# Layer norms' inverse deviation: ScalarE square root and VectorE reciprocal, or a ScalarE copy and a GpSimd power

## The chip, the core and the metric

The kernel runs on one core of a Trainium2 chip. It is written in Bass with the Tile framework. The engines are named as the profile names them: PE (TensorE matmul) and PEld (its weight loads), DVE (VectorE), ACT (ScalarE), POOL (GpSimd) and SP (SyncE, which issues DMAs). The metric is the device time of one execution in microseconds, the median of several runs.

## The reference

A batch of 4 images of 192 channels and 64 x 64 pixels, all in 32-bit floats, goes through four layers:

```python
# layer 0: per pixel over the 192 channels
xn = layer_norm(x)                          # (x - mu) * rsqrt(var + 1e-5) * g + b
q = deform_conv(xn, w_p, b_p, w_d)          # offsets by a 3x3 convolution, bilinear gather of 9 taps
k, v = l2norm(split(qkv(xn)))
x = x + proj(softmax(q @ k.T * temperature) @ v)    # attention over channels, 6 heads
x = x + gelu(layer_norm(x) @ w_fc1 + b) @ w_fc2 + b
# layer 1: attention over all 4096 pixels, 96 channels
x = x + W(softmax(theta(x).T @ phi(x)) @ g(x).T)
# layer 2: 8x8 windows at stride 6, 6 heads
y = qkv(layer_norm(x))
x = x + hft(proj(fold(window_attention(y))))        # hft: sigmoid of a depthwise 3x3, times its input
z1, z2 = split(gelu(fc1(layer_norm(x))))
x = x + fc2(z1 * dwconv3(layer_norm(z2)))
# layer 3: a depthwise 3x3 with weights computed from the image's mean
out = depthwise(x, weights(mean(x)))
```

Every `layer_norm` takes mean and variance over the channels of one pixel. These five norms (layer 0's first and second, layer 2's first, second and the one of its gate `z2`) are what the change touches.

## The kernel before

Channels lie on the partitions, pixels along the free dimension. The channels of a pixel are thus summed by a matmul with a matrix of 1/192 (or 1/384), and each norm is the same chain of steps over a block of pixels:

- PE: mean into PSUM (`pm`); DVE: difference `d`; ACT: square `sq`.
- PE: `variances`, four groups of matmuls that put the variance of a quarter of the block into 32 partitions each (`pv`), so that 512 pixels make a tile of 128 x 128.
- ACT: `r = sqrt(pv + eps)`, read from PSUM, written to SBUF.
- DVE: `r = 1 / r`.
- PE: `spread_quarters`, which spreads `r` back over all partitions (`pb`); DVE: `d * pb`.

`layer_norm_steps` (L354) yields after each step: MEAN, DIFFERENCE, SQUARE, VARIANCE (after ACT's square root) and INVERSE (after the reciprocal), so that callers can place the steps among other work. It serves layer 0's first norm (`offsets`, tiles `r_l`, 8 blocks per image, 128 columns) and layer 2's first norm (`windows`, tiles `r_l2n`, 11 rows of windows per image, mostly 96 columns). `norm_steps` in `mlp0` (tiles `r_l0m`, 8 per image, 128 columns), `pair_norm_steps` (tiles `r_l2n` at L1365, 4 per image, 256 columns) and `gate_variance` in `mlp` (tiles `rz`, 8 per image, 128 columns, with the reciprocals at L1661 and L1667) are the same chain for other layouts.

The images run through these stages, in program order:

- `offsets(0)` and `gather(0)`: layer 0's first norm, the offset convolution and 297 indirect DMAs issued by POOL (L572), with the offsets of image 1 woven into it (`woven=True`); then `mlp0(0)` alone.
- For each image b: `keys` (for b = 1 and 2 with the offsets of image b + 1 woven in), `layer1` with the gather of image b + 1 woven in, `windows`, and `rest`: `project`, `mlp` and `layer3` of image b, into which `mlp0(b + 1)` is woven in parts. For the last image nothing is woven in.

The Tile framework's planner orders instructions by their costs and priorities, except under `tc.manual_schedule()`, where each engine keeps the order of the program. `windows` and `mlp` (with the parts of `mlp0` that run within it) are written under it. In `windows`, three groups of windows make a row. In group 0 the norm of the row after next runs up to its square; after group 1's second pair come its variance, square root and reciprocal (`norm(wr + 2, INVERSE)`, L1284); group 2 begins with the scores of the next group (L1112), and then spreads the result (`norm(wr + 2)`, L1267). In POOL's queue lie the copies into `xs`, `qs`, `ks`, `qw`, `xw` (L1064 to L1091) and the additions at L1199. In `mlp`, the order around the gate norm is

```python
gate_difference(hi)
widen(j, (1,))          # matmuls, then Gelu on ACT
gate_variance(lo)       # variances, then the square root on ACT
gate_square(hi)
widen(j, (2,))
...                     # depthwise taps on DVE
nc.vector.reciprocal(r[lo], r[lo])
gate_variance(hi)
... # means of the next pair's norm
nc.vector.reciprocal(r[hi], r[hi])
```

The compiler puts a table load (ACT_TABLE_LOAD) ahead of an ACT instruction whose function is not in the table set that is loaded. The functions used here are Square, Sqrt, Identity, Copy, Gelu, Exp and Sigmoid.

Of the kernel before, what the change touches and what calls it, by code (L numbers as in the profile page):

```python
# [12 lines left out]
AF = mybir.ActivationFunctionType  # L13
ALU = mybir.AluOpType
# [65 lines left out]
def conv_seq_kernel(ctx: ExitStack, tc: tile.TileContext, a, out: bass.AP):  # L80
    nc = tc.nc
# [11 lines left out]
    def const(shape, name):  # L93
        return wpool.tile(shape, F32, tag=name, name=name)
# [8 lines left out]
    V, VW = {}, {}  # L103
# [53 lines left out]
    for w in range(2):  # L157
        to = pixels[:, :, STRIDE * w : STRIDE * w + WS]
        nc.gpsimd.tensor_add(to, to, ident[:, bass.ts(w, WS * WS)].rearrange("p (r c) -> p r c", c=WS))
    eps = const([128, 1], "eps")  # L160
    nc.gpsimd.memset(eps, 1e-5)
    headmask = const([P, P], "headmask")
# [188 lines left out]

    MEAN, DIFFERENCE, SQUARE, VARIANCE, INVERSE = range(5)

    def layer_norm_steps(src, n, dst, sb, ps, name, affine=None, rows=None, tag="v", bufs=2, own=""):  # L354

        pm = ps.tile([128, 512], F32, tag="n", name=f"pm_{name}")[:P, :n]
        for k in range(2):
            nc.tensor.matmul(pm, lhsT=mean192, rhs=src[:, k, :], start=k == 0, stop=k == 1)  # L360
        yield MEAN
        d = sb.tile([P, 2, 512], F32, tag=f"ln_d{own}", name=f"d_{name}", bufs=bufs)[:, :, :n]
        dst = d if dst is None else dst
        nc.vector.tensor_tensor(d, src, pm.unsqueeze(1).to_broadcast([P, 2, n]), ALU.subtract)
        yield DIFFERENCE
        sq = sb.tile([P, 2, 512], F32, tag=f"ln_sq{own}", name=f"sq_{name}")[:, :, :n]
        nc.scalar.activation(sq, d, AF.Square)
        yield SQUARE
        pv = ps.tile([128, 512], F32, tag=tag, name=f"pv_{name}", bufs=1)[:, 0 : n // 4]
        variances(pv, sq, mean192)  # L370
        r = sb.tile([128, 128], F32, tag="ln_r", name=f"r_{name}", bufs=2)[:, 0 : n // 4]
        nc.scalar.activation(r, pv, AF.Sqrt, bias=eps)
        yield VARIANCE
        nc.vector.reciprocal(r, r)
        yield INVERSE
        pb = spread_quarters(r, n, P, ps, name)
        for k in range(2):
            of, to, r = d[:, k, :], dst[:, k] if rows else dst[:, k, :], pb
            if rows:
                of, r = (t.rearrange("p (r c) -> p r c", r=rows) for t in (of, r))  # L380
            if affine is None:
                nc.vector.tensor_tensor(to, of, r, ALU.mult)
            else:
                nc.vector.tensor_tensor(of, of, r, ALU.mult)
                nc.scalar.activation(to, of, AF.Identity, bias=affine[1][:, k], scale=affine[0][:, k])
        return dst
# [18 lines left out]
    def offsets(b, pool, kept=None, woven=False):  # L405
# [19 lines left out]
        with ExitStack() as s:  # L425
            sb = s.enter_context(pool_of(name="l0a", bufs=1 if woven else 2))
            s1 = s.enter_context(pool_of(name="l0a1", bufs=1))
            ps = s.enter_context(pool_of(name="l0aps", bufs=2, space=PSUM))
            for i in range(NCH):
                xi = sb.tile([P, 2, CN], F32, tag="xi", name=f"xi_{b}_{i}", bufs=2)  # L430
                nc.sync.dma_start(out=xi, in_=given(b)[:, :, bass.ts(i, CN)])
                layer_norm(
                    xi, CN, xnv[:, :, 1 + 8 * i : 9 + 8 * i, 1:65], sb, ps, f"l0_{b}_{i}",
                    affine=(V["l0_g1"], V["l0_b1"]), rows=8,
                )
                yield

# [257 lines left out]
    def mlp0(b, m2, pool, sb, ps):  # L695
# [58 lines left out]
        def norm_steps(x, i):  # L754

            pm = ps.tile([128, CN], F32, tag="n", name=f"pm_l0m_{b}_{i}")
            nc.tensor.matmul(pm, lhsT=mean_all[:, 0, :], rhs=x[:, 0:CN], start=True, stop=False, skip_group_check=True)
            for q in range(2):
                nc.tensor.matmul(
                    pm[:, bass.ts(q, HN)], lhsT=mean_all[:, 1 + q, :], rhs=x[:, CN:], start=False, stop=True,  # L760
                    skip_group_check=True,
                )
            yield MEAN
            d = sb.tile([M, 3 * HN], F32, tag="wide_d", name=f"d_l0m_{b}_{i}", bufs=2)
            over(d, x, pm, ALU.subtract)
            yield DIFFERENCE
            sq = sb.tile([M, 3 * HN], F32, tag="wide_sq", name=f"sq_l0m_{b}_{i}")
            nc.scalar.activation(sq, d, AF.Square)
            yield SQUARE
            pv = ps.tile([128, CN], F32, tag="v", name=f"pv_l0m_{b}_{i}", bufs=1)[:, 0:128]  # L770
            for j in range(4):
                to = pv[32 * j : 32 * j + 32, :]
                nc.tensor.matmul(to, lhsT=mean_all[:, 0, 0:32], rhs=sq[:, bass.ts(j, 128)], start=True, stop=False)
            for j in range(4):
                to, at = pv[32 * j : 32 * j + 32, :], CN + 128 * (j % 2)
                nc.tensor.matmul(to, lhsT=mean_all[:, 1 + j // 2, 0:32], rhs=sq[:, at : at + 128], start=False, stop=True)
            r = sb.tile([128, 128], F32, tag="ln_r", name=f"r_l0m_{b}_{i}", bufs=2)
            nc.scalar.activation(r, pv, AF.Sqrt, bias=eps)
            yield VARIANCE
            nc.vector.reciprocal(r, r)  # L780
            yield INVERSE
            over(d, d, spread_quarters(r, CN, M, ps, f"l0m_{b}_{i}"), ALU.mult)
            return d
# [555 lines left out]
    def pair_norm_steps(x, j, sb, ps, name):  # L1339

        lo, hi = of_pair(x, j)
        pms = [ps.tile([128, CN], F32, tag="n", name=f"pm_{name}_{h}") for h in range(2)]
        for h in range(2):
            nc.tensor.matmul(pms[h], lhsT=mean_all[:, 0, :], rhs=lo[:, h], start=True, stop=False)
        for h in range(2):
            nc.tensor.matmul(pms[h], lhsT=mean_all[half(h), 0, :], rhs=hi[half(h)], start=False, stop=True)
        yield MEAN
        d = sb.tile([M, 3, CN], F32, tag="ln_d", name=f"d_{name}")
        for h in range(2):
            nc.vector.tensor_tensor(d[:, h], lo[:, h], pms[h], ALU.subtract)  # L1350
            nc.vector.tensor_tensor(d[half(h), 2], hi[half(h)], pms[h][half(h)], ALU.subtract)
        yield DIFFERENCE
        sq = sb.tile([M, 3, CN], F32, tag="ln_sq", name=f"sq_{name}")
        nc.scalar.activation(sq, d, AF.Square)
        yield SQUARE

        pv = ps.tile([128, CN], F32, tag="v", name=f"pv_{name}", bufs=1)[:, 0:HN]
        for k in range(2):
            for g in range(4):
                nc.tensor.matmul(  # L1360
                    pv[32 * g : 32 * g + 32, :], lhsT=mean_all[:, (1 + g // 2) * k, 0:32],
                    rhs=sq[:, 2 if k else g // 2, bass.ts(g % 2, HN)], start=k == 0, stop=k == 1,
                )
        r = sb.tile([128, HN], F32, tag="ln_r2", name=f"r_{name}")
        nc.scalar.activation(r, pv, AF.Sqrt, bias=eps)  # L1365
        yield VARIANCE
        nc.vector.reciprocal(r, r)
        yield INVERSE
        for h in range(2):
            pb = ps.tile([128, CN], F32, tag="n", name=f"pb_{name}_{h}")  # L1370
            for g in range(2):
                nc.tensor.matmul(pb[:, bass.ts(g, HN)], lhsT=spread[:, 2 * h + g, :], rhs=r, start=True, stop=True)
            nc.vector.tensor_tensor(d[:, h], d[:, h], pb, ALU.mult)
            nc.vector.tensor_tensor(d[half(h), 2], d[half(h), 2], pb[half(h)], ALU.mult)
        return d
# [120 lines left out]
    def mlp(b, x, sums, sb, ps, taps, hn):  # L1496


        with ExitStack() as s:
# [6 lines left out]
            n = 2 * 3 * (UR + 2) * (W + 2)  # L1506
# [8 lines left out]
            r, sqs, accs = {}, {}, {}  # L1515
# [33 lines left out]
            def gate_variance(i):  # L1549
                pv = ps.tile([128, 512], F32, tag="n", name=f"pvz_{b}_{i}")[:, 0:128]  # L1550
                variances(pv, sqs.pop(i), mean384)
                r[i] = s1.tile([128, 128], F32, tag="zr", name=f"rz_{b}_{i}", bufs=2)
                nc.scalar.activation(r[i], pv, AF.Sqrt, bias=eps)

            def gate_scale(i):
                z2 = z2s.pop(i)
# [69 lines left out]
            with tc.manual_schedule():  # L1626
                for j in range(pairs):
                    lo, hi, upper, lower = 2 * j, 2 * j + 1, j - 1, j - 2
# [29 lines left out]
                    widen(j, (2,))  # L1658
                    if upper >= 0:
                        upper_taps(upper, 1)  # L1660
                    nc.vector.reciprocal(r[lo], r[lo])  # L1661
                    gate_variance(hi)
                    norm = None
                    if j + 1 < pairs:
                        norm = pair_norm_steps(x, j + 1, sb, ps, f"l2n2_{b}_{j + 1}")
                        links(norm, MEAN)
                    nc.vector.reciprocal(r[hi], r[hi])  # L1667
                    if norm is not None:
                        links(norm, SQUARE)
                    if upper >= 0:  # L1670
# [187 lines left out]
    with ExitStack() as s:  # L1858
        sb = s.enter_context(pool_of(name="l0first", bufs=1))
# [137 lines left out]
```

## Time and profile before

| what | value |
|---|---|
| time, median of 3 runs | 6844.52 us (6835.98 to 6856.77) |
| profiled execution: span | 6951.6 us |
| profiled execution: time | 6951.6 us (the span, no other time is on record for it) |
| mean granted TensorE clock | 0.938 |
| instructions | 115213 |
| HBM | 628 MB read, 106 MB written |

The profile is of one execution. PE, DVE, ACT and POOL are busy for a share of the span; register, branch, semaphore and DMA-issuing instructions are not counted. Groups of instructions are shown with their line, engine, operation, names of tiles (output<-inputs) and shapes, then their busy time, the mean duration of one in ns, and the idle time of the engine just before them with what ended it. The chain of waits is followed back from the last instruction, at each step to what released it. The stages of the first image lie at 0 to 632 us (offsets and gather), 632 to 858 (`mlp0`), 858 to 1615 (`keys`, `layer1`), 1615 to 1898 (`windows`) and 1898 to 2392 (`rest`).

### The profile page before, as it was taken

To read this page: it belongs to the slowest core of one execution; us is meant where nothing else is said; L and a number is where in the kernel's file an instruction comes from. 1 tells how busy PE (TensorE), PEld (TensorE's weight loads), DVE (VectorE), ACT (ScalarE), POOL (GpSimd) and SP (SyncE) were. 2 spreads that over 40 slices of the span, in tenths; PEclk is the share of its full clock that TensorE was granted. 3 is DMA by queue.
4 is the path that set the end of the run, shared out by engine and by line. 5 is a ranking of instruction groups with operands and counts; after the bars stand their busy time and mean duration, and the time that the engine had idled before them with its cause. 6 is when DMAs were issued, how large, how long until landed. Compare 5 with 4: busy or idle time off the path is not lost.

```text
span 6951.6 us, 115213 instructions
## 1 busy us (share of the span) xinstructions
PE 6255.4 (90%) x45188; PEld 4235.5 (61%) x45188; DVE 4817.8 (69%) x7087; ACT 3725.4 (54%) x6214; POOL 2061.6 (30%) x2273
## 2 busy tenths in 40 slices
PE   7677999999988899999988899999998889999876
PEld 4445578886643468886654458887554457766432
DVE  3664279985577769985586849996576757765656
ACT  3664368874544358874544348885544325545331
POOL 2654057752200047761200017772210000012100
PEclk8888989999999999999989999999998979999988
DMA  7795257751010277762010067673110010010000
GB/s 229 257 317 180 70 161 225 226 180 36 21 28 13 62 237 227 220 214 57 11 42 12 21 216 217 220 222 102 32 29 22 14 52 10 14 36 12 7 3 20
DMA packets 362109, 743.45 MB, mean 107 GB/s; under 512 B 52647, under 2 KB 245335, under 8 KB 360798
## 3 DMA queue, kind: packets, MB, share of 16 engines
q0 software_dynamic: 95616, 469.38, 21.1%
q1 hardware_dynamic: 265950, 266.70, 12.9%
q8 instruction: 356, 5.83, 0.4%
q14 instruction: 187, 1.53, 0.1%
HBM read 628.06 MB, written 106.21 MB: 106 GB/s over the span
## 4 chain that ended last, share of the span: by engine, by line
PE 65%; DVE 17%; ACT 7%; issue 4%; DMA 4%; SPq 1%; another core or an unknown queue 1%; POOL 1%; DVEq 0%; ACTq 0%; POOLq 0%
PE s L920 11%; PE y L986 11%; PE h L590 7%; PE v L1151 2%; DVE ha L1328 2%; PE qk L1076 2%; PE h L1528 2%; DMA ring<-table,idx 2%; PE qk L1077 2%; DVE ga L1328 2%; PE po L482 2%; PE t L1159 1%; PE h L803 1%; DVE gate L1328 1%; PE zm L1539 1%
## 5 line engine op out<-in xcount | busy, mean ns | idle before, releaser
L572 POOL DMA_INDIRECT ring<-table,idx x1188 | 1657.7, 1395 | 1103.3 <-DVE row L579 273.2
L920 PE MATMUL s<-ths,ph 96*128 96x256 f32 x4096 | 981.6, 385 | 14.2 <-ACT ths L914 7.4
L920 PEld LDWEIGHTS s<-ths,ph 96*128 96x128 f32 x4096 | 782.8, 193 | 154.8 <-ACT ths L914 19.0
L578 ACT ACTIVATE row<-ring,pos 128x384 f32<-128x384 f32 x1188 | 697.7, 609 | 213.5 <-DVE xo L583 132.4
L579 DVE SCALAR_TENSOR_TENSOR row<-ring,fr,row 128x384 f32<-128x384 f32 x1188 | 696.9, 611 | 84.1 <-ACT row L578 56.8
L986 PE MATMUL y<-sc,gx 128*97 128x256 f32 x3008 | 720.1, 379 | 0.0
L582 ACT ACTIVATE xo<-row,pos 128x192 f32<-128x192 f32 x1188 | 504.6, 448 | 151.3 <-remote 73.1
L986 PEld LDWEIGHTS y<-sc,gx 128*97 128x97 f32 x3008 | 489.0, 164 | 125.7 <-issue 2.3
L583 DVE SCALAR_TENSOR_TENSOR xo<-row,fr,xo 128x192 f32<-128x192 f32 x1188 | 464.4, 411 | 106.9 <-ACT xo L582 59.6
L590 PE MATMUL h<-ti,xo 128*128 128x192 f32 x2376 | 460.3, 329 | 5.6 <-DVE xo L583 5.6
L922 ACT COPY sc<-s 128x1024 f32<-128x1024 f32 x376 | 377.3, 1003 | 164.1 <-PE s L920 155.1
L983 DVE TENSOR_TENSOR sc<-sc,mbs 128x1024 f32<-128x1024 f32 x376 | 446.7, 1216 | 20.9 <-ACT mbs L946 13.7
L927 DVE TENSOR_TENSOR top<-top,sc 128x1024 f32<-128x1024 f32 x282 | 344.5, 1222 | 149.5 <-ACT sc L922 133.9
L590 PEld LDWEIGHTS h<-ti,xo 128*128 128x128 f32 x2376 | 404.4, 191 | 40.4 <-DVE xo L583 11.7
L984 ACT ACTIVATE sc<-sc 128x1024 f32<-128x1024 f32 x376 | 392.5, 1053 | 39.2 <-DVE sc L983 36.6
L1135 DVE TENSOR_REDUCE es<-ex 128x6 f32<-128x384 f32 x264 | 133.3, 546 | 358.8 <-ACT ex L1131 358.8
L590 PE MATMUL h<-kept,xo 128*128 128x192 f32 x990 | 261.9, 402 | 121.4 <-DVE xo L583 61.7
L1569 POOL COPY gate<-gate 128x192 f32<-128x192 f32 x12 | 4.2, 351 | 1115.2 <-ACT gate L1562 1115.2
L590 PEld LDWEIGHTS h<-kept,xo 128*128 128x128 f32 x990 | 191.2, 226 | 203.6 <-DVE xo L583 92.9
L1328 DVE SCALAR_TENSOR_TENSOR ga<-gate,v,ga 128x1024 f32<-128x1024 f32 x234 | 299.7, 1281 | 7.2
L986 PE MATMUL y<-se,gx 128*97 128x256 f32 x1088 | 260.4, 379 | 0.5 <-ACT yn L992 0.5
L1533 ACT ACTIVATE z<-h,bias_fc1T 128x512 f32<-128x512 f32 x192 | 118.0, 687 | 230.2 <-PE h L1530 229.9
(390 smaller groups left out, 11548.6 us busy)
## 6 DMA issues: line engine op xcount, KB each, us to landing
ti<-table SPq DMA_DIRECT2D x396, 96.0 KB
table<-tt SPq DMA_DIRECT2D x24, 1056.0 KB
ring<-table,idx POOLq DMA_INDIRECT x1188
xnd<-xn SPq DMA_DIRECT2D x4, 3270.0 KB
table<-kept SPq DMA_DIRECT2D x12, 1056.0 KB
table<-tt SPq DMA_DIRECT2D x44, 288.0 KB
xi<-in_x_dram SPq DMA_DIRECT2D x32, 384.0 KB
xk<-xd SPq DMA_DIRECT2D x32, 384.0 KB
```

Of the source, the lines that this page charges most:

```text
L572: nc.gpsimd.indirect_dma_start(out=gt.rearrange("p r q c -> p (r q c)"), out_offset=None, in_=table[:, :], in_offset=bass.IndirectOffsetOn ...
L578: nc.scalar.activation(row, gt[:, :, 0, :], AF.Copy, scale=pos[:, t, 9 + tap : 10 + tap])
L579: nc.vector.scalar_tensor_tensor(row, gt[:, :, 1, :], fr[:, t, 9 + tap : 10 + tap], row, ALU.mult, ALU.add)
L582: nc.scalar.activation(xo[:, j, :], row[:, 0, :], AF.Copy, scale=pos[:, t, tap : tap + 1])
L583: nc.vector.scalar_tensor_tensor(xo[:, j, :], row[:, 1, :], fr[:, t, tap : tap + 1], xo[:, j, :], ALU.mult, ALU.add)
L590: nc.tensor.matmul(acc[m // 2][:, bass.ts(m % 2, C)], lhsT=xo.rearrange("p j c -> p (j c)")[:, bass.ts(m, 128)], rhs=tt, start=t == 0 and ...
L920: nc.tensor.matmul(p[:, t, :], lhsT=ph[:, bass.ts(G * g + t, 128)], rhs=ths[i], start=True, stop=True)
L922: nc.scalar.copy(to, p)
L983: nc.vector.tensor_tensor(ex, ex, mbs[i].unsqueeze(1).to_broadcast([128, G, QN]), ALU.add)
L984: nc.scalar.activation(ex, ex, AF.Exp)
L986: nc.tensor.matmul(py, lhsT=gx[:, G * g + t, :], rhs=ex[:, t, :], start=g == 0 and t == 0, stop=g == NG - 1 and t == G - 1,)
L1328: nc.vector.scalar_tensor_tensor(acc[:, b], src(tap, b), w[:, tap : tap + 1], acc[:, b], ALU.mult, ALU.add)
```

## The change

The step "square root on ACT, reciprocal on DVE" becomes "copy with bias on ACT, power of -0.5 on POOL". Two helpers, `take` and `invert`, stand for the two steps. A tile of -0.5 in each partition is filled once by POOL and read as a second operand with a stride of zero. All five norms use the new form except the offsets of image 1 that are woven into the first gather (`power=not woven`), so 148 of 156 norms change. Layer 3's square root and the square roots of `l2norm` stay as they are. The places of the two steps in the program order are kept.

```diff
+    minus_half = const([128, 1], "minus_half")
+    nc.gpsimd.memset(minus_half, -0.5)
...
+    def take(to, pv, power=True):
+
+        nc.scalar.activation(to, pv, AF.Identity if power else AF.Sqrt, bias=eps)
+
+    def invert(to, power=True):
+
+        if power:
+            nc.gpsimd.tensor_tensor(to, to, minus_half.to_broadcast([128, to.shape[-1]]), ALU.pow)
+        else:
+            nc.vector.reciprocal(to, to)
+
-    def layer_norm_steps(src, n, dst, sb, ps, name, affine=None, rows=None, tag="v", bufs=2, own=""):
+    def layer_norm_steps(src, n, dst, sb, ps, name, affine=None, rows=None, tag="v", bufs=2, own="", power=True):
...
-        nc.scalar.activation(r, pv, AF.Sqrt, bias=eps)
+        take(r, pv, power)
         yield VARIANCE
-        nc.vector.reciprocal(r, r)
+        invert(r, power)
         yield INVERSE
...
-                    affine=(V["l0_g1"], V["l0_b1"]), rows=8,
+                    affine=(V["l0_g1"], V["l0_b1"]), rows=8, power=not woven,
...
# norm_steps of mlp0, and pair_norm_steps:
-            nc.scalar.activation(r, pv, AF.Sqrt, bias=eps)
+            take(r, pv)
             yield VARIANCE
-            nc.vector.reciprocal(r, r)
+            invert(r)
             yield INVERSE
...
# gate_variance, and the two places of the gate's reciprocal:
-                nc.scalar.activation(r[i], pv, AF.Sqrt, bias=eps)
+                take(r[i], pv)
...
-                    nc.vector.reciprocal(r[lo], r[lo])
+                    invert(r[lo])
...
-                    nc.vector.reciprocal(r[hi], r[hi])
+                    invert(r[hi])
```

More of the change, by code (lines that the diff above doesn't have):

```diff
@@ L1364, in pair_norm_steps @@
         r = sb.tile([128, HN], F32, tag="ln_r2", name=f"r_{name}")
-        nc.scalar.activation(r, pv, AF.Sqrt, bias=eps)
+        take(r, pv)
         yield VARIANCE
-        nc.vector.reciprocal(r, r)
+        invert(r)
         yield INVERSE
```

## The prediction

> **What bounds the kernel now.** I read the page first, then the chain of waits, then the groups by shape, then two stretches of the chain in order of time.
>
> ```profile
> PE 6255.4 (90%) x45188; PEld 4235.5 (61%) x45188; DVE 4817.8 (69%) x7087; ACT 3725.4 (54%) x6214; POOL 2061.6 (30%) x2273
> ...
> PE 65%; DVE 17%; ACT 7%; issue 4%; DMA 4%; SPq 1%; another core or an unknown queue 1%; POOL 1%; DVEq 0%; ACTq 0%; POOLq 0%
> ```
>
> PE is the bound; what the change can win is PE's idle time, and only where a norm causes it. The busy time by stage shows where that idle time lies (columns: PE, PEld, DVE, ACT, POOL busy us, granted clock, DMA share, GB/s): a windows stage, then the stage of layer 2's rest woven with layer 0's MLP.
>
> ```profile
> 1615.00:1898.00 283.00, 261.13 (x5072) 172.70 (x5070) 169.25 (x240) 148.18 (x273) 73.29 (x202) 1.00 0.10 28
> 1898.00:2392.00 494.00, 413.67 (x1840) 212.74 (x1841) 383.93 (x485) 202.39 (x284) 11.57 (x38) 0.91 0.10 28
> ```
>
> In the windows 22 us of PE are idle, in the rest 80 us. POOL, which gets the new work, is nearly empty in the rest. The groups by shape name what is removed from ACT:
>
> ```profile
> L816 ACT ACT_TABLE_LOAD x47 | 60.3, 1283 | 164.5 <-PE h L810 164.0
> L372 ACT ACT_TABLE_LOAD x43 | 55.2, 1283 | 2.0 <-PE pv_l L339 1.3
> L1131 ACT ACT_TABLE_LOAD x40 | 51.3, 1283 | 0.7
> L778 ACT ACT_TABLE_LOAD x32 | 41.1, 1283 | 0.6
> L1533 ACT ACT_TABLE_LOAD x32 | 41.1, 1283 | 104.2 <-PE h L1530 98.5 <-DVE ha L1479 5.3
> L1553 ACT ACT_TABLE_LOAD x32 | 41.1, 1283 | 0.6
> ```
>
> With the smaller groups there are 265 loads, each of 1.283 us, whenever the square root alternates with Gelu, Exp or Sigmoid. The chain in order of time shows which of them PE feels. In the gate norm of the rest:
>
> ```profile
> 2052.43 1.28 ACT L1553
> ...
> 2055.48 1.28 ACT L1533
> ...
> 2058.06 1.28 ACT L1553
> 2059.34 0.01 issue
> 2059.36 0.38 ACT rz L1553
> 2059.73 0.04 issue
> 2059.78 2.08 PE pm_l2n L1344 x2
> ```
>
> Three loads stand in a row on the chain, and PE waits for the copy that frees the PSUM bank. In the windows it is different (timeline):
>
> ```profile
> 1723.03 1.28 ACT L372 ACT_TABLE_LOAD   x1
> ...
> 1724.53 0.34 ACT L372 ACTIVATE r_l2n<-pv_l2n,eps 128x96 f32<-128x96 f32 x1 [0.22 <-PE pv_l2n L339]
> ...
> 1724.90 0.75 DVE L374 RECIPROCAL r_l2n<-r_l2n 128x96 f32<-128x96 f32 x1 [1.03 <-ACT r_l2n L372]
> 1725.71 0.76 PEld L348 LDWEIGHTS pb_l2n<-r_l2n,spread 128*96 128x96 f32 x8 [0.54 <-DVE r_l2n L374]
> ```
>
> Here the load runs while ACT waits for the variance anyway; what PE waits for is the square root and the reciprocal, with only the 0.91 us of scores (L1112) as cover.
>
> **What goes.** The instruction list of the changed program holds 56 loads: 214 go, 5 come (four for layer 3's own square root, one for the offsets woven into the first gather, which keep it). That is 209 x 1.283 = 268 us of ACT. DVE loses 148 reciprocals: 24 of 32 at L374 with 128 columns (22.8 us), 44 narrower ones (32.3), 32 at L780 (30.3), 16 at L1367 (28.0), 32 at L1661 and L1667 (30.4), together 144 us. The copy with bias costs what the square root cost, 0.34 to 0.47 us.
>
> **What comes: 148 powers on POOL, the unknown price.** No row shows a power. From below, POOL's own add:
>
> ```profile
> L1199 POOL TENSOR_TENSOR ot<-ot,ot 96x128 f32<-96x128 f32 x40 | 23.2, 581 | 0.3
> ...
> L374 DVE RECIPROCAL r_l<-r_l 128x128 f32<-128x128 f32 x32 | 30.4, 951 | 65.5 <-ACT r_l L372 63.0 <-issue 2.5
> ```
>
> POOL copies of 528 and 16 columns take 637 and 197 ns: a base of 183 ns, 0.86 ns per column. The adds (315 ns for 64 columns, 581 for 128) give 2.06 to 3.1 ns per column. A function costs more: DVE's reciprocal grows by (1751-951)/128 = 6.25 ns per column, DVE's addition by 1.04, a factor of 6. A power is a logarithm and an exponential; I take twice that factor, so 12 x 2.06 = 24.7 ns per column. With the base: 2.55 us for 96 columns, 3.34 for 128, 6.5 for 256. The low end is the add (0.48, 0.58, 0.97), the high end twice my value per column (4.9, 6.5, 12.8). I take the middle because the reciprocal is the nearest row in kind.
>
> The GPSIMD Engine Reference of the Trainium skill (Performance versus the Vector engine) speaks against the change: elementwise work on GpSimd takes about twice VectorE's time; applied to the reciprocal as an estimate that gives 1.9 us for 128 columns, and the sum below would come out near zero, about 6855. The trace has such a factor for the add alone (581 ns against DVE's 284).
>
> **The sum, site by site** (low / middle / high, us of the profiled execution).
>
> *Windows*, 44 norms. The handover to POOL should cost what that to DVE costs (0.03 us after the copy, 0.06 before PE). PE already idles 0.41 us at the spread, so each row pays the power less 0.753: -12 / +79 / +183. Rows 0 and 2 of each batch wait 0.7 and 0.83 us for a load that goes: -6. On POOL the power stands behind the qw and xw copies, which end 3.9 us earlier; behind it wait the xs copies (0.42 us), read only in the next row. No DMA is moved; the first gathers of batches 0, 2 and 3 stand behind eight powers on POOL, but need the offsets, which come later still. Sum -18 / +73 / +177.
>
> *First MLP alone* (632 to 858), 8 norms. The copy comes 2.34 us after the variance, 1.31 of them the load. Then 0.37, the reciprocal, the spread 3.75 us after the variance, just when PE is free. Changed: 1.48 plus the power, so up to 2.27 us are hidden by L828 and L825. PE idles 11 us in the whole stage, so I count half as the most to win: -5 / +8 / +34.
>
> *Offsets*, 24 norms. In batch 0 the spread starts 0.06 us after the reciprocal, with PE idle 0.2: 8 x (power - 0.95). In batches 2 and 3 the mean slack is 0.35, and the planner now puts fewer matmuls between variance and spread: 16 x (power - 1.3). Sum -4 / +52 / +128.
>
> *Gate norms*, 32. Slack from reciprocal to spread is mostly 7 to 16 us, so the power hides. The gain is the trio of loads: PE idles 2.98 us in 10 of the 16 stretches, 2.72 in two and 0.4 to 0.6 in the rest, 37 us in all: -37 in each case.
>
> *Layer 2's second norm* (L1365), 16, 256 columns, reciprocal 1.75 us. In batches 0 to 2 the four norms of a batch have slack 0.06, 0.15, 3.27 and 0.15; loads of 1.3, 2.6, 1.3 and 1.3 us go from before the copy. With 6.5 us that is +3.5, +2.1, +0.2, +3.5, or 9 per batch; the last batch, where DVE delays the reciprocal by 1 to 2 us, +7. Sum -20 / +35 / +136.
>
> *Layer 0's norm in the rest*, 24: the load (1.3) and DVE's queue (0.9 to 5.3 us before the reciprocal starts) go, slack is 1.4 to 30 us at five of eight: -13 / 0 / +33. Loads on the chain elsewhere: -3.
>
> Total -100 / +128 / +468 on a profiled time of 6951.6 us (one execution, the span is its whole time; the median of the runs is 0.9846 of it). In device time -98 / +126 / +461: 6746, 6970, 7305. The sum crosses zero near 12.6 ns per column, a power of 1.8 us for 128 columns.
>
> **Rivals.** (1) *The power is cheap*: below 1.8 us for 128 columns the gate and the second norm decide. For it: POOL copies run at 0.86 ns per column, so a dozen pipelined steps would fit. Against it: the add alone takes 2 to 3 ns. At the add's price 6746, faster. (2) *POOL is the new bound of the norms*: a software loop without overlap, 6.5 us and more per power, 7305; the last pair of gate norms and the MLP norms with slack under 2 us then stall too. (3) *The loads do not go*: would hold if the copy needed a table set of its own; the list of 56 loads rules it out. (4) *ACT's saved time has no effect*, since PE is 90% busy: near zero only with rival 1's border price, 6840 to 6860.
>
> **Numbers.** Forecast (power dearer than 2 us, slower) 0.53, of which 0.15 for rival 2's region; rival 1, 0.42; between them, within 0.3%, 0.05. A measurement of this kernel can tell about 0.3%. The range goes from rival 1's end, 6750, towards rival 2's, 7240, which leaves out about 1 in 10 above and less below; the slower case alone spans 6870 to 7305.
>
> **What would show it.** ACT_TABLE_LOAD falls to 56 and ACT busy by some 268 us, DVE by 144, POOL rises by 148 powers (about 510 us at my price). Right: a POOL row of about 3.3 us for 128 columns, PE idle before pb_l2n of some 2.2 us per row, windows stages longer by 18 us each, the gate's trio gone. Wrong: a power under 1.8 us, windows no longer than before, the rest stages 10 to 20 us shorter each.

## The result

The kernel after takes 9636.29 us (median of 4 runs, 9627.98 to 9669.98), beside 6840.25 (6816.69 to 6856.77) before: a ratio of 1.411, 95% interval 1.407 to 1.415. It is 41% slower. The forecast was slower, 6970 us with a range to 7240: the sign was right, the size far outside.

The profiled execution after has a span of 9668.1 us. Its busy times and the share of the engines in the chain of waits:

```profile
PE 6483.4 (67%) x45188; PEld 4404.7 (46%) x45188; DVE 4696.3 (49%) x6939; ACT 3452.3 (36%) x6005; POOL 5256.8 (54%) x2422
...
PE 44%; POOL 32%; DVE 9%; issue 7%; ACT 4%; DMA 4%; SPq 1%; DVEq 0%; ACTq 0%; POOLq 0%
```

POOL was 1% of the chain and is now a third of it, though it is busy for only 54% of the span. So over the whole span POOL is not a bound; its powers are a latency that PE waits for. ACT lost 273 us (268 worked out) and DVE 121 (144 worked out; why 23 less stays open). PE, with the same 45188 matmuls, is busy 228 us longer; nothing in the prediction accounts for that.

The powers, by shape (busy, mean ns of one, idle time of POOL before it and what ended it):

```profile
L363 POOL TENSOR_TENSOR rz<-rz,minus_half 128x128 f32<-128x128 f32 x32 | 674.8, 21100 | 481.5 <-ACT rz L358 481.5
...
L363 POOL TENSOR_TENSOR r_l2n<-r_l2n,minus_half 128x256 f32<-128x256 f32 x16 | 664.9, 41554 | 117.9 <-ACT r_l2n L358 117.9
L363 POOL TENSOR_TENSOR r_l2n<-r_l2n,minus_half 128x96 f32<-128x96 f32 x36 | 562.6, 15628 | 140.3 <-ACT r_l2n L358 140.3
...
L363 POOL TENSOR_TENSOR r_l2n<-r_l2n,minus_half 128x80 f32<-128x80 f32 x8 | 104.9, 13118 | 19.3 <-ACT r_l2n L358 19.3
```

From 80 to 256 columns a power grows by (41554 - 13118) / 176 = 162 ns per column, on a base of 0.19 us; for 128 columns 21.1 us were measured. Where POOL was idle before a power, ACT's copy ended the idle time: 118 of the 148 powers start when their input is there. The other 30 stand in POOL's queue. The second power of each gate pair starts 17 to 18 us after its input, behind the first (16 powers); three of layer 2's second norm start 14 us late and six of layer 0's MLP norm 30 to 39 us late, behind other powers; five in the windows start 2.3 to 2.9 us late, behind cheap work of POOL's own. One row of the windows (timeline), where the prediction showed the square root and the reciprocal:

```profile
1994.78 0.34 ACT L358 ACTIVATE r_l2n<-pv_l2n,eps 128x96 f32<-128x96 f32 x1 [1.30 <-PE pv_l2n L341]
...
1995.20 15.62 POOL L363 TENSOR_TENSOR r_l2n<-r_l2n,minus_half 128x96 f32<-128x96 f32 x1 [4.19 <-ACT r_l2n L358]
...
2010.87 1.59 PE L350 MATMUL pb_l2n<-r_l2n,spread 128*96 128x96 f32 x8 [15.31 <-POOL r_l2n L363]
```

The table load is gone, the handover costs 0.08 us, and PE waits 15.31 us. The list of waits has this at every site (line waited for: us in total, times, longest):

```profile
PE pb_l2n L350 <- POOL r_l2n L363: 664.1, 44, 18.4
PE pb_l2n L1385 <- POOL r_l2n L363: 629.8, 16, 44.9
PE pb_l0m L350 <- POOL r_l0m L363: 514.5, 29, 22.3
PE pb_l L350 <- POOL r_l L363: 483.7, 24, 21.4
PE pb_z L350 <- POOL rz L363: 474.6, 32, 18.6
```

The five rows add up to 2767 us; the span grew by 2716. The two are not the same thing: PE's idle time grew by 2488 us (696 to 3185; the new waits stand in place of some old ones), and its busy time by the 228. Last, the two stages by time, as shown for before (the column after POOL is the granted clock):

```profile
1888.00:2364.00 476.00, 299.07 (x5061) 199.19 (x5060) 160.94 (x227) 119.55 (x251) 236.13 (x202) 0.76 0.05 15
2369.00:3219.00 850.00, 433.08 (x1848) 230.25 (x1847) 369.64 (x471) 158.55 (x252) 514.84 (x58) 0.73 0.06 17
```

Windows went from 283 us to 476, the rest from 494 to 850. And the clock fell: 0.76 and 0.73, where it was 1.00 and 0.91. In the windows PE was busy 261 us for the same work and is now busy 299.

### The profile page after: what moved, and what is told of

It is laid out like the page before. It is cut to its first block, busy times and chain, and to the rows that moved or that the text cites. A ratio compares the mean times of both kernels' runs of the same rounds, so it can differ in the third digit from the quotient of the medians.

```text
span 9668.1 us, 115155 instructions
## 1 busy us (share of the span) xinstructions
PE 6483.4 (67%) x45188; PEld 4404.7 (46%) x45188; DVE 4696.3 (49%) x6939; ACT 3452.3 (36%) x6005; POOL 5256.8 (54%) x2422
## 4 chain that ended last, share of the span: by engine, by line
PE 44%; POOL 32%; DVE 9%; issue 7%; ACT 4%; DMA 4%; SPq 1%; DVEq 0%; ACTq 0%; POOLq 0%
POOL r_l2n L363 14%; PE s L933 8%; PE y L999 7%; POOL r_l0m L363 6%; POOL r_l L363 5%; POOL rz L363 5%; PE h L603 4%; DMA ring<-table,idx 2%; PE v L1164 1%; PE o L838 1%; PE po L495 1%; PE h L1541 1%; DVE ga L1341 1%; PE rb L1238 1%; PE t L1172 1%
## 5 line engine op out<-in xcount | busy, mean ns | idle before, releaser
L585 POOL DMA_INDIRECT ring<-table,idx x1188 | 1680.8, 1415 | 796.0 <-DVE row L592 195.3
L363 POOL TENSOR_TENSOR r_l2n<-r_l2n,minus_half 128x96 f32<-128x96 f32 (+2 forms) x60 | 1332.4, 22207 | 277.6 <-ACT r_l2n L358 277.6
L363 POOL TENSOR_TENSOR rz<-rz,minus_half 128x128 f32<-128x128 f32 x32 | 674.8, 21100 | 481.5 <-ACT rz L358 481.5
L363 POOL TENSOR_TENSOR r_l0m<-r_l0m,minus_half 128x128 f32<-128x128 f32 x32 | 674.5, 21077 | 409.2 <-ACT r_l0m L358 409.2
L363 POOL TENSOR_TENSOR r_l<-r_l,minus_half 128x128 f32<-128x128 f32 x24 | 497.2, 20718 | 270.1 <-ACT r_l L358 270.1
L350 PE MATMUL pb_l2n<-r_l2n,spread 128*96 128x96 f32 (+1 forms) x352 | 69.9, 380 | 664.1 <-POOL r_l2n L363 664.1
L1385 PE MATMUL pb_l2n<-r_l2n,spread 128*128 128x256 f32 x128 | 60.3, 652 | 629.8 <-POOL r_l2n L363 629.8
```

The source lines that it names most:

```text
L363: nc.gpsimd.tensor_tensor(to, to, minus_half.to_broadcast([128, to.shape[-1]]), ALU.pow)
L585: nc.gpsimd.indirect_dma_start(out=gt.rearrange("p r q c -> p (r q c)"), out_offset=None, in_=table[:, :], in_offset=bass.IndirectOffsetOn ...
```

## The experiments

Two theories were tested first: that the power's own duration is the loss, and that it lies in handing the norm to POOL at all (its queue, its semaphores). The lower clock came up as a third in the second experiment below. Differences are of medians unless they are said to be by the ratio, which comes with an interval.

**1. A cheap operation in the power's place.**

```diff
-            nc.gpsimd.tensor_tensor(to, to, minus_half.to_broadcast([128, to.shape[-1]]), ALU.pow)
+            nc.gpsimd.tensor_tensor(to, to, minus_half.to_broadcast([128, to.shape[-1]]), ALU.mult)
```

> The changed kernel with POOL's multiply in place of its power at all 148 norms (this leaves the power -0.5 out of the computation); queues, hand-overs, table loads and buffers stay as in the changed kernel. Theory 1 (the execution time of the power itself, 162 ns per column, is the whole loss, and the site-by-site sum was sound apart from that price): POOL's rows fall to about 0.58 us for 128 columns, PE's waits for POOL from 2770 us to under 100, the granted clock returns to about 0.94, and the time is that of the sum's low end, 6746 us (6720 to 6790), 1.4% below the kernel before. Theory 2 (handing the norm to POOL's queue costs, behind its copies, its gathers and its semaphores, whatever the operation): POOL remains the releaser of PE's waits at the spreads and the time stays above 7000 us.

Measured: 6735.8 us, before 6817.1; ratio 0.9877 (0.9848 to 0.9906). That is the low end of the prediction's sum (6746) within 10 us, with the same queues and handovers; as a difference it is -81 us (-64 to -104 by the interval) beside -98. Handing the norm to POOL costs little by itself, so the theory of the queue falls as the root: the powers that queue up above do so behind other powers. PE's waits for POOL at the spreads are some 57 us; POOL's multiply takes 0.35 to 0.85 us, and 1.16 for 256 columns.

**2. The power on an eighth of the columns**, which puts its duration near the one I had assumed.

```diff
+            n = to.shape[-1] // 8
-            nc.gpsimd.tensor_tensor(to, to, minus_half.to_broadcast([128, to.shape[-1]]), ALU.pow)
+            nc.gpsimd.tensor_tensor(to[:, 0:n], to[:, 0:n], minus_half.to_broadcast([128, n]), ALU.pow)
```

> The changed kernel with the power on one eighth of the columns of each norm only (the other columns are left as variances): with 0.19 us and 162 ns per column a power takes 2.1 us for 96 columns of a norm, 2.8 for 128, 5.4 for 256, near the price that the prediction took for the whole. Theory 1 (only the price of the power was wrong, the site sums hold): windows +53 us, first MLP +4, offsets +38, gate norms -37, layer 2's second norm +20, other -3: +75 us, 6914 us. Theory 2 (a power on POOL also slows others, so that the site sums are too low): 7000 us or more.

Measured: 7130.09 us, ratio 1.045 (1.0407 to 1.0493), so +313 us (+307 by the ratio) where +75 was expected. The powers took 2.28, 2.9 to 3.3 and 5.9 us (for 12, 16 and 32 columns), a little more than estimated; with these the same site sum gives +93. Over 200 us are missing from it. The gate norms are not where: at 3.3 us a power, PE has no wait for POOL at their spread. Part of them is seen in the busy time, in steps of 3 us around one spread of the windows (PE waits 1.96 us up to 1655.79; the clock is the number after POOL's):

```profile
1652.00:1655.00 3.00, 1.38 (x64) 1.10 (x64) 1.24 (x4) 1.07 (x2) 1.52 (x1) 1.00 0.02 5
1655.00:1658.00 3.00, 2.21 (x27) 1.86 (x27) 2.93 (x5) 0.32 (x1) 1.54 (x8) 0.93 0.00 0
1658.00:1661.00 3.00, 3.00 (x40) 2.17 (x40) 1.12 (x4) 0.48 (x1) 0.00 (x0) 0.50 0.03 5
...
1682.00:1685.00 3.00, 3.00 (x6) 1.36 (x5) 0.00 (x0) 0.58 (x1) 0.87 (x3) 0.52 0.00 0
1685.00:1688.00 3.00, 3.00 (x94) 2.09 (x93) 1.18 (x3) 1.78 (x4) 2.15 (x8) 1.00 0.02 5
```

From 1657.6, 1.8 us after the wait, the clock is 0.50 for 27 us, and PE is busy for nearly all of it: this wait is paid a second time, in slow matmuls. The offsets of batches 2 and 3 (one stage each) run at 0.75 and take 129 and 130 us in place of 85 and 80.

**3. Matmuls that nobody reads in PE's wait**, in the kernel of 2.

```diff
+                            keep_warm(ps2.tile([128, 512], F32, tag="a", name=f"fill_{b}_{wr}")[:, 0:384], 3)
                             norm(wr + 2)
```

> The kernel with the power on one eighth of the columns, which took 7130 us where the sum gave 6914, with three matmuls that nobody reads put in front of the spread in each row of the windows stages, where PE otherwise idles about 2.1 us for the power. In that kernel the windows stages last 335 to 342 us (293 to 301 in the kernel with the power at the gate alone), and the granted clock falls to 0.50 for some 25 us after such a wait. Theory 1 (PE's idling of 2 us itself brings the half clock, and that is the missing part): the clock in the windows stages goes from 0.87 back to 0.98 or more, these stages last 310 to 318 us, the time falls by about 90 us to 7040 us. Theory 2 (POOL's power slows PE in another way, or the clock falls for another reason): the clock in the windows stages stays at 0.87 and the time at 7130 us or above.

Measured: 7022.91 us, ratio 1.0276 (1.0237 to 1.0315), 107 us less than in experiment 2 (119 by the ratios) for additional work. The windows stages take 307, 307, 307 and 314 us, the clock in the first is 0.97, where 0.98 or more was expected.

**4. The wait without POOL:** before, with the reciprocal three times in a row at the norms of the windows.

```diff
-        nc.vector.reciprocal(r, r)
+        for _ in range(3 if tag == "n" else 1):
+            nc.vector.reciprocal(r, r)
```

> The kernel before with VectorE's reciprocal taken three times in a row at the 44 norms of the windows, so that PE waits about 1.9 us there in place of 0.41 us, without POOL and with every table load in place. Theory 1 (the length of PE's wait alone brings the half clock): the four windows stages get about 40 us longer each, as with the power on one eighth of the columns, of which 16 us each are the two added reciprocals; 6975 us in all, and the clock in these stages falls to about 0.87. Theory 2 (the half clock comes with the work on POOL): the wait alone, 44 x 1.5 = 66 us, 6885 us, with the clock at 0.98 to 1.00.

Measured: 7022.17 us, ratio 1.0283 (1.0244 to 1.0322): +183 us (+193 by the ratio), above both figures, on the side of the clock. The waits at these spreads grew by 63 us only. The timeline, PE alone:

```profile
1699.72 1.57 PE L348 MATMUL pb_l2n<-r_l2n,spread 128*96 128x96 f32 x8 [2.07 <-DVE r_l2n L375]
1701.22 1.55 PE L1152 MATMUL v<-qkvT,xw 96*64 96x96 f32 x16
...
1710.90 0.89 PE L1152 MATMUL v<-qkvT,xw 96*64 96x96 f32 x16
```

The same sixteen matmuls take 1.55 us just after the wait and 0.89 us nine microseconds later. POOL has no part in it.

**5. A shorter wait:** the same with two reciprocals in place of three.

```diff
-        nc.vector.reciprocal(r, r)
+        for _ in range(2 if tag == "n" else 1):
+            nc.vector.reciprocal(r, r)
```

> The kernel before with the reciprocal taken twice in a row at the 44 norms of the windows (this leaves the inversion out there): PE's wait at the spread goes from 0.41 to about 1.16 us, between the 0.41 that keeps the full clock and the 2.07 that halves it for some 6 us. If the clock falls only after waits near 2 us: 44 x 0.75 = 33 us more, 6873 us, and after the spread the eight matmuls take 0.9 us as in the kernel before. If any wait near 1 us brings the half clock: about half of what three reciprocals cost, 90 us more, 6930 us.

Measured: 6907.36 us, ratio 1.0107 (1.0073 to 1.0141), +74 us, between the two expectations. Counting in the traces shows why. In 36 rows of the windows the spread is followed by sixteen `v` matmuls; from the start of the first to that of the twelfth takes 0.48 us at the full clock and 0.86 at half:

| kernel | mean wait at the spread, us | rows at half clock behind it |
|---|---|---|
| multiply (1) | 0.04 | 0 of 36 |
| before | 0.45 | 5 of 36 |
| reciprocal twice (5) | 1.33 | 15 of 36 |
| power on an eighth (2) | 1.89 | 31 of 36 |
| reciprocal three times (4) | 2.09 | 36 of 36 |
| after | 14.97 | 36 of 36 |
| power on an eighth, filled (3) | none | 0 of 36 |
| after, filled (6) | 0.81 | 0 of 36 |

Four more kernels with a mean wait of 0.38 to 0.49 us (those of experiments 7 to 10) have 3 to 10 such rows of 36. So there is no sharp threshold of the wait: the number of half-clock rows rises with it from about 0.4 us to 2 us.

What it goes with in a single row can be read from the clock records of the traces; no run set it on its own. In all twelve the clock is either 1.0 or 0.5, and it changes only at the edges of steps of 3.41 us: every stretch at one clock lasts a whole number of such steps, to within 0.1% of a step. Three steps of experiment 2, around the wait shown there:

```profile
1654.19:1657.60 3.41, 1.81 (x25) 1.60 (x26) 3.34 (x5) 0.00 (x0) 2.35 (x8) 1.00 0.00 0
1657.60:1661.01 3.41, 3.41 (x41) 2.45 (x42) 1.53 (x4) 0.80 (x2) 0.00 (x0) 0.50 0.02 5
...
1684.91:1688.32 3.41, 3.41 (x99) 2.22 (x101) 1.50 (x3) 2.02 (x4) 2.24 (x8) 1.00 0.02 5
```

Counted over the twelve traces, by PE's busy share in a step and the clock of the step behind it:

| clock in the step | PE busy in it | steps | half clock in the next |
|---|---|---|---|
| full | under 40% | 828 | 828 |
| full | 40 to 80% | 2066 | 504 |
| full | over 80% | 18294 | 10 |
| half | under 70% | 2149 | 2149 |
| half | 70 to 90% | 426 | 351 |
| half | over 90% | 1962 | 695 |

So it matters where a wait falls among the steps. In experiment 5 the waits are nearly all alike, most of them 1.28 us; the 21 rows at full clock are those in which the wait ended 1.0 to 2.2 us after the start of a step, the 15 at half clock those in which it ended within 0.6 us of the start or 2.9 us and more behind it. The 15 us of the kernel after empty whole steps, wherever they fall. What holds the clock at half through steps in which PE is busy for over 90% stays open.

**6. The wait filled in the kernel after:** as in 3, with 22 matmuls.

```diff
+                            keep_warm(ps2.tile([128, 512], F32, tag="a", name=f"fill_{b}_{wr}")[:, 0:384], 22)
                             norm(wr + 2)
```

> The changed kernel with 22 matmuls that nobody reads in front of the spread in each row of the windows stages, where PE otherwise idles some 15 us for the power. The spread waits for the same power. Windows stages last 481 to 488 us in the changed kernel, of which 11 x 15 = 165 us are the waits. Theory 1 (the rest of their growth is the half clock after each wait): these stages get 20 to 30 us shorter, their clock goes from 0.76 to 0.95 or more, and the time falls by 80 to 120 us to about 9540 us. Rival (the waits are all there is): 9636 us or, where the matmuls delay the spread, more.

Measured: 9514.76 us against 9636.29 (121 us less; the ratios to before are 1.3925, 1.388 to 1.397, and 1.411). The windows stages take 451 to 461 us in place of 481 to 488, at this clock:

```profile
1895.00:2330.00 435.00, 393.31 (x5436) 250.26 (x5436) 160.99 (x227) 119.56 (x251) 227.79 (x201) 0.96 0.06 16
```

**7. The power at the gate norms alone**, the other sites with square root and reciprocal.

```diff
-    def layer_norm_steps(src, n, dst, sb, ps, name, affine=None, rows=None, tag="v", bufs=2, own="", power=True):
+    def layer_norm_steps(src, n, dst, sb, ps, name, affine=None, rows=None, tag="v", bufs=2, own="", power=False):
...
# norm_steps of mlp0, and pair_norm_steps:
-        take(r, pv)
+        take(r, pv, False)
         yield VARIANCE
-        invert(r)
+        invert(r, False)
```

> The power only at the 32 gate norms in layer 2's rest; every other norm has ScalarE's square root and VectorE's reciprocal as before. The prediction took these 32 as hidden by 7 to 16 us of slack and gaining 37 us. Theory 1 (they are hidden only while a pair's two powers in a row stay under the slack; at 21.1 us each they do not): the waits at the gate's spread (pb_z) stay near the 475 us of the changed kernel, the time is about 470 us longer than before, 7310 us. Rival (the wait at pb_z in the changed kernel is work that other late powers pushed in front of it; alone they hide): 6803 us.

Measured: 7280.79 us (one run), before 6817.1: +464. The prediction counted these 32 norms as hidden, at -37. The list of waits:

```profile
PE pb_z L350 <- POOL rz L363: 474.8, 32, 18.6
```

The spread of a pair's first norm waits 8.6 to 15 us, that of the second 18.6 us each time, as in the kernel after (8.5 to 15 and 18.6).

**8. The removed loads alone:** ACT's copy stays, DVE's reciprocal comes back.

```diff
-            nc.gpsimd.tensor_tensor(to, to, minus_half.to_broadcast([128, to.shape[-1]]), ALU.pow)
+            nc.vector.reciprocal(to, to)
```

> The changed kernel with VectorE's reciprocal in place of POOL's power (this leaves the square root out of the computation): ScalarE copies the variance, 209 table loads are gone, the rest stands as in the kernel before. It prices the removed loads alone. Theory 1 (the loads are on the path only at the places that the prediction named: gate norms 37 us, windows 6, layer 2's second norm about 18, the rest small): about 68 us less of 6840, 6773 us. Rival (ScalarE's time is worth nothing because PE is 90% busy): 6840 us, no change. Rival (all 268 us of loads are on the path): 6575 us.

Measured: 6764.39 us, ratio 0.9903 (0.9869 to 0.9937): 53 us less by the medians (66 by the ratio, 43 to 89 by its interval), 68 expected. Neither nothing nor all 268 us.

**9. The price by shape**, with powers that nobody waits for, in the kernel before.

```diff
...
+                if i % 2 == 1:
+                    for m, n in (((128, 128), (1, 128)), ((32, 128), (16, 128)), ((128, 32), (128, 16)), ((128, 1), (64, 128)))[i // 2]:
+                        nc.gpsimd.tensor_tensor(unread[:m, :n], ones[:m, :n], minus_half[:m].to_broadcast([m, n]), ALU.pow)
```

> The kernel before with 32 powers on POOL whose result nobody reads, after the gate's strip copies in layer 2's rest, in eight shapes: 128 partitions with 128, 32, 16 and 1 columns, and 128 columns with 64, 32, 16 and 1 partitions. It measures the price. If the price goes by columns alone (162 ns each, whatever the partitions): 21, 5.4, 2.8, 0.35 us, and 21 us for each of the four narrow ones. If it goes by elements (1.26 ns each over all partitions): 10.5, 5.4, 2.8 and 0.35 us for 64, 32, 16 and 1 partitions. The time itself, with nobody waiting, is expected within 1% of the kernel before; more, if powers on POOL slow VectorE or delay POOL's own copies.

```profile
L1578 POOL TENSOR_TENSOR unread<-ones,minus_half 128x128 f32<-128x128 f32 x4 | 85.4, 21338 | 0.2
...
L1578 POOL TENSOR_TENSOR unread<-ones,minus_half 1x128 f32<-1x128 f32 x4 | 83.0, 20752 | 0.3
...
L1578 POOL TENSOR_TENSOR unread<-ones,minus_half 128x16 f32<-128x16 f32 x4 | 12.6, 3153 | 0.3
L1578 POOL TENSOR_TENSOR unread<-ones,minus_half 128x1 f32<-128x1 f32 x4 | 6.3, 1584 | 0.0
```

The price goes by columns: one partition costs what 128 do. A single column took 1.58 us where the line from wider tiles gives 0.35; why stays open. These 32 powers add 468 us to POOL, and the time was 6861.16 (one run, before 6839.4, 6800.58 to 6857.23): within the 1% expected. That is 22 us above the median, so powers that nobody waits for cost little, which agrees with experiment 1.

**10. A version that beats both:** before, with the copy by ACT at the gate norms only, and there nine cheap instructions on POOL in place of the power: a first guess from the number's bits, then two Newton steps. The part of the edit at the power, against the kernel after (`y` and `t` are two tiles of POOL's own):

```diff
...
+            yi = y.bitcast(I32)
+            nc.gpsimd.tensor_scalar(yi, to.bitcast(I32), -0.5, 1597463007.0, ALU.mult, ALU.add)
+            for k in range(2):
+                nc.gpsimd.tensor_tensor(t, y, y, ALU.mult)
+                nc.gpsimd.tensor_tensor(t, t, to, ALU.mult)
+                nc.gpsimd.tensor_scalar(t, t, -0.5, 1.5, ALU.mult, ALU.add)
+                nc.gpsimd.tensor_tensor(to if k else y, y, t, ALU.mult)
-            nc.gpsimd.tensor_tensor(to, to, minus_half.to_broadcast([128, to.shape[-1]]), ALU.pow)
...
```

> The variance copied by ScalarE at the 32 gate norms only, and there the inverse square root worked out on POOL from multiplies and adds: a first guess from the number's bit pattern, taken as an integer, and two Newton steps, nine instructions of 0.3 to 0.85 us, 5 to 6 us per norm in place of 21.1. The other norms stay as in the kernel before. Theory 1 (below the slack of 7 to 16 us the power hides and the three table loads of each pair go from the path): 37 us less, about 6780 us where the kernel before takes 6817. Rival (two such chains in a row, 11 us, exceed the slack at some pairs, or the loads come back at other places): 6800 to 6880 us.

Measured: 6790.3 us, before 6839.4; ratio 0.9925 (0.9894 to 0.9955). The nine instructions average 0.39 to 0.67 us, together 4.4 us, and PE waits next to nothing for them:

```profile
PE pb_z L348 <- POOL rz L369: 7.4, 4, 2.8
```

49 us less by the medians (31 to 72 by the interval), 37 expected: clear of the noise, though under 1%. The cover of the gate norms was as predicted, for an operation that fits under it.

## Why the prediction was wrong, step by step

**The term that failed is the price of the power.** "A power is a logarithm and an exponential; I take twice that factor" gave 24.7 ns per column; measured were 162, 6.5 times that, and 3.3 times the high end. The base (0.18 against 0.19) and the linear growth were right. The fault is in how the upper end was made: it was twice my own middle value, and no row of the trace limits an operation that the trace does not have. The add's 2.06 was also the lowest of its readings; the two adds named there differ by (581 - 315) / 64 = 4.2 ns per column, which accounts for a factor of 2 of the 6.5. Forecast and rival 2 were the same mechanism, and its open end should have been open in the range. That the sign came out right rests on a guess at the price, made at 0.53, and is in part luck.

The GPSIMD Engine Reference of the Trainium skill (Performance versus the Vector engine) gives about twice VectorE's time for elementwise work. Here a power takes 21.1 us and the reciprocal that it replaces 0.951: 22 times. That section measures an add, and does not carry over to a function.

**The site sums held at the cheap end, and in part at the dear one.** At a cheap price they gave 6746, and experiment 1 measured 6735.8. At the measured price, by the same formulas: windows 36 x (15.63 - 0.753) + 8 x (13.12 - 0.66) - 6 = 629; offsets 8 x (20.7 - 0.95) + 16 x (20.7 - 1.3) = 468; first MLP 8 x (21.1 - 2.27) = 151; layer 2's second norm, by the covers that its four norms had (16 x 41.55 less 3 x 16.7 and 19), 596; together 1844. The rest is worked out only now. The gate pairs, with two powers of 21.1 less 11.5 of slack, the middle of the 7 to 16, give 16 x 30.7 - 37 = 454. For layer 0's norm in the rest there was no formula, and the waits show 514 - 151 = 363; six of these 24 powers stood 30 to 39 us behind other powers on POOL, which the prediction did not reckon with for them. With the -3 elsewhere that is 2658 us, of 2716 by the span and 2796 by the medians. That it comes so close is in part luck: the sum is one of idle time, and PE's idle time grew by 2488 us only; the 228 us of slower matmuls, which it does not hold, make up the difference.

**"Gate norms: the power hides, -37 in each case"** was false as an unconditional step. The cover is 7 to 16 us, and the second power of a pair stands behind the first on POOL: of its 21.1 us PE waits for 18.6. By that cover it would not have held everywhere at my high end (2 x 6.5 us), though at the middle price it did, in experiment 2. Experiment 7 measured +464, experiment 10 a gain of 49 at 4.4 us per norm, which agrees with the trio of loads and its 37 us.

**A step was missing: PE's clock.** The sum charged each wait once. Experiments 2 to 6 show a second charge of the same order or above while waits are short: at 2 us, 44 norms of the windows cost +183 us where their added waits are 63. Had the power cost what I assumed, the result would by experiment 2 have been near 7130 and not 6970. The kernel before had a sign of it: it already runs matmuls that nobody reads (`keep_warm`, at L854, L995 and L1240 to L1244). In the kernel after the clock is the smaller part: PE is busy 337 us longer than in experiment 1 (6483 against 6146) for the same matmuls, at work under the half clock for 1210 us where it was 473, and the fill of the windows alone returned 121 us.

The Trainium skill has the rule in "TensorE: Matmul & The Clock Gate" (HAM oscillation — how this bites in real kernels): gaps longer than about 3.4 us bring the half clock. Here gaps of 2.1 us brought it in all 36 rows and gaps of 1.3 us in 15 of 36, so the rule's direction agrees and its figure, as a limit of the gap, does not; 3.41 us is here the step in which the clock changes.

**Loads and ACT.** 56 loads, as counted. That they lie on the path at the gate and at little else held: 53 us by experiment 8 against 68. Rival 4 (ACT's time without effect) falls, rival 3 too. Rival 1's premise, a cheap power, was wrong; the time it gave for an operation at the add's price was right to 10 us, by experiment 1.

**The scale from profile to runs.** The profiled execution of before lay 111 us above the median. Its stretch from the first indirect DMA to the first matmul of `keys` took 745 us, and 690 to 698 in experiments 4, 5, 7 and 10, which leave it as it was: part of that execution's extra time came from no change, so the span of after beside it understates the loss.

## What to carry to other kernels

A function on POOL is not priced by POOL's adds and copies: measure it alone, unread, before it is put between two matmuls; and the price of the power went by columns, so spread the values over the partitions and keep the columns few. Price a new wait of PE twice when it exceeds some 1 us, once as idle time and once as the slow matmuls behind it, and look at the granted clock by stage and around the wait. Where two powers follow each other on POOL, the second has the first in front of it. Where a table load is in the way, take it out only where the replacement fits under the slack, as the gate norms do with 4.4 us under 7 to 16.

## What was not expected of the hardware

POOL's power of 128 columns takes 20.8 us on one partition and 21.3 on 128, about 162 ns per column; the same on a tile of ones as on variances (21.3 and 21.1). A short wait of PE halves its clock for far longer than the wait: 2 us of idling went with 6.8 us of half clock in one place (experiment 4, 1698.6 to 1705.4) and 27.3 us in another (experiment 2, from 1657.6), with PE at work for most of it. The clock changes in steps of 3.41 us, and went to half after every step with PE busy for under 40% (828 of 828); so of waits of 1.28 us some halve it and some do not, by where they end among the steps. A few matmuls that nobody reads, in the wait, prevent it in all 36 rows.
